# Third batch's normalised rows: transposed by VectorE in 32x32 pieces and brought through DRAM, or by TensorE

## The chip, the cores and the metric

One core of a Trainium2 chip. The time is device microseconds of one launch of the whole kernel. Engines: PE (TensorE, matrix multiply), DVE (VectorE), ACT (ScalarE), POOL (GpSimd) and SP (SyncE, whose queue issues nearly all DMAs here). Each runs its own instructions in order and waits on semaphores for the others.

## What is computed

One transformer block on 4 batches of 512 tokens by 512 features, in float32. Layer normalisation, causal attention with rotary positions (32 query heads of 16 features, 8 key and value heads), a residual, a second layer normalisation, a gated MLP with 1376 hidden features, a second residual.

```python
def reference(resid, Wq, Wk, Wv, Wo, W_gate, W_up, W_down):
    x = resid                                   # (4, 512, 512)
    n = layernorm(x)
    q, k, v = rope(n @ Wq), rope(n @ Wk), n @ Wv
    x = x + softmax(causal(q @ k.T) / 4) @ v @ Wo
    n = layernorm(x)
    return x + (silu(n @ W_gate.T) * (n @ W_up.T)) @ W_down.T
    ...
```

## The kernel before, in words

The kernel writes out the order of every engine's instructions by hand: the Python code runs step by step, and each step appends instructions to the queues. Batches are counted from 0 here, so the third batch is b = 2 and the fourth is b = 3.

*Projections of a batch* (`projections`, L328). A batch's rows come as four tiles of 128 tokens by 512 features, `xa`, by DMA (L338). For each tile:
- `measure` (`statistics`, L196): on DVE the statistics (L200), their aggregate (L201) and the variance plus epsilon (L202), then on POOL the power -1/2 (L203);
- `norm` (`normalised`, L206): for b > 1 a small DVE operation (L210) and the normalisation itself on ACT (L211), in place in `xa`;
- the transposition into `xnT`, which has the features on the partitions, since PE contracts over partitions.

There are two ways to transpose. `transposed` (L255) has PE transpose four blocks of 128x128 into a PSUM bank (L258) and copies the bank to `xnT`, on ACT (L263) or at times on DVE (L261). `flipped` (L265) has DVE transpose all 32x32 blocks of the tile at once into a buffer `xt` (L268; two such buffers), writes it to a DRAM tensor `flip` with the blocks in their places by four DMAs of 64 KB (L272), and reads the columns of the tile before back into `xnT` by one DMA of 256 KB (L274); at the last tile it reads two. All these DMAs are on SP's queue.

Before, batches 0 and 2 go by `transposed` and batches 1 and 3 by `flipped`.

After that come the products on PE: `rest` has 48 portions of four matmuls each or their like (L253): 8 for keys, 8 for the first quarter of the queries, 8 for values, 24 for the other queries. A finished bank is rotated by DVE (a shuffle, L304, and a product, L308) and POOL (L305, L309).

*Attention of a batch* (`slot`). A batch has 8 head groups, and each group is a round of four visits and a last visit. In a visit PE makes scores (L553 and L566) into two pairs of PSUM banks, ACT takes the exponential (L654), POOL applies the causal mask (L659), and DVE finds minima of negated scores for the group two ahead (L599). At the end of a round DVE transposes the minima (L639), SP takes them through DRAM into the masked queries `qa` of a later group (L640, L649, L651), POOL makes the next `qa` (L538), and PE multiplies the exponentials by the values (`averages`, L681).

Between visits, `gap` fills PE with portions from a list of (cost, step): it runs steps until their summed cost reaches the visit's share of the total. Beside it, `odd_steps` takes DVE steps from the queue `aside` as long as a visit's budget of microseconds lasts; `measure`, `norm` and `flip` steps are in that queue. Attention of batch 0 is `slot(0, ...)`, and its list holds the rest of batch 1's products, batch 2's `turned` steps and products, then batch 3's `begin`, `turned` and half of its products. A `turned` step (`tail`) waits in the order of the program until its tile's `flip` step has been taken from `aside`, taking steps if need be, and then calls `transposed` where the batch goes that way.

`begin` of a batch issues the four loads of its rows (unless done) and puts its steps into `aside`. Batch 2's loads are issued earlier, at the end of batch 1's last `flip`; batch 3's are issued where `begin3` stands in the list. The four `xa` buffers are shared: batch 3's rows go into those that batch 2's rows leave.

Of the kernel before, what the change touches and what calls it, by code (L numbers as in the profile page):

```python
# [22 lines left out]
NT = T // P  # L23
# [51 lines left out]
def preln_block_kernel(  # L75
# [65 lines left out]
    def values(n):  # L141

        return homes[n][:, 8:11, :].rearrange("p a c -> p (a c)").rearrange("p (j g d) -> p j g d", j=NT, g=NKV)
# [9 lines left out]
    flip = [dram.tile([D, T], F32, name=f"flip{n}") for n in range(2)]  # L153
# [35 lines left out]
    def put(step):  # L189
        held.append(step) if holding[0] else step()  # L190

    def release():
        while held:
            held.popleft()()

    def statistics(src):  # L196
        st = small.tile([P, 6], F32, tag="st", name="st")
        mv = small.tile([P, 2], F32, tag="mv", name="mv")
        rstd = small.tile([P, 1], F32, tag="rstd", name="rstd")
        nc.vector.bn_stats(st, src)  # L200
        nc.vector.bn_aggr(mv, st)  # L201
        nc.vector.tensor_scalar(rstd, mv[:, 1:2], EPS, None, ALU.add)  # L202
        nc.gpsimd.tensor_tensor(rstd, rstd, neghalf, ALU.pow)  # L203
        return src, mv, rstd

    def normalised(dst, found, by_act=False):  # L206
        src, mv, rstd = found
        if by_act:
            shift = mv[:, 1:2]
            nc.vector.tensor_scalar(shift, mv[:, 0:1], rstd, -1.0, ALU.mult, ALU.mult)  # L210
            put(lambda: nc.scalar.activation(dst, src, AF.Identity, bias=shift, scale=rstd))  # L211
        else:
            nc.vector.tensor_scalar(dst, src, mv[:, 0:1], rstd, ALU.subtract, ALU.mult)
# [3 lines left out]
    aside, later = deque(), deque()  # L217
# [47 lines left out]
    def flipped(xn, i, n, dst, last=NT - 1):  # L265

        t = work.tile([P, D], F32, tag="g", name="xt", bufs=2)
        nc.vector.transpose(t, xn)  # L268
        turned = flip[n].rearrange("(c d) (i r s) -> i r d c s", d=32, r=4, s=32)
        for r in range(4):  # L270
            rows = t[32 * r : 32 * r + 32, :]
            nc.sync.dma_start(out=turned[i, r], in_=rows.rearrange("d (c s) -> d c s", s=32))  # L272
        for a in [i - 1, i] if i == last else [i - 1] if i > 0 else []:
            nc.sync.dma_start(out=dst[:, :, ts(a, P)], in_=flip[n].rearrange("(k p) t -> p k t", p=P)[:, :, ts(a, P)])  # L274
# [24 lines left out]
    def rotated(ps, dst, engine=nc.gpsimd):  # L299

        rot = work.tile([P, T], F32, tag="rot", name="rot", bufs=4)

        def sines():
            nc.vector.stream_shuffle(rot, ps, ROTATE)  # L304
            put(lambda: engine.tensor_tensor(rot, rot, sin, ALU.mult))  # L305

        def cosines():
            nc.vector.tensor_tensor(dst, ps, cos, ALU.mult)  # L308
            put(lambda: engine.tensor_tensor(dst, dst, rot, ALU.add))  # L309

        return [(0.73, sines), (0.69, cosines)]

    def both_steps(measure, norm, flip, tiles=range(NT), norm_us=0.6, flip_us=0.75):

        for i in tiles:
            yield 1.05, lambda i=i: measure(i)
            for a in [i - 1, i] if i == NT - 1 else [i - 1] if i > 0 else []:
                yield norm_us, lambda a=a: norm(a)
                yield flip_us, lambda a=a: flip(a)

    def both_steps_apart(measure, norm, flip, flip_us):

        steps = {"m": (1.05, measure), "n": (0.2, norm), "f": (flip_us, flip)}
        for kind, i in ("m0", "m1", "n0", "m2", "f0", "n1", "m3", "f1", "n2", "n3", "f2", "f3"):
            cost, step = steps[kind]
            yield cost, lambda step=step, i=int(i): step(i)

    def projections(b, n, early=False, then=None):  # L328

        home, xa, found, xn, ready = homes[n], {}, {}, {}, []  # L330
        xnT = xnT_of[b]

        def load(i):
            if early:
                xa[i] = xr[b, i]
            else:
                xa[i] = work.tile([P, D], F32, tag="xa", name="xa", bufs=4)
                nc.sync.dma_start(out=xa[i], in_=x[b, ts(i, P), :])  # L338

        def measure(i):  # L340
            found[i] = statistics(xa[i])

        def norm(i):
            xn[i] = work.tile([P, D], F32, tag="xa", name="xa", bufs=4) if early else xa[i]
            normalised(xn[i], found[i], by_act=b > 1)

        def flip(i):
            if b > 1:
                release()
            if b % 2:  # L350
                flipped(xn[i], i, 1, xnT)
            ready.append(i)
            if i == NT - 1 and then:
                then()

        def keys():
            def finish(ps):
                kr = work.tile([P, T], F32, tag="rot", name="kr", bufs=4)

                def spread():  # L360
                    release()
                    ks = work.tile([P, T], F32, tag="rot", name="ks", bufs=4)
                    nc.vector.stream_shuffle(ks, kr, SWAP)
                    for t, hf, src in ((0, 0, kr), (1, 1, kr), (0, 1, ks), (1, 0, ks)):
                        put(
                            lambda t=t, hf=hf, src=src: nc.gpsimd.tensor_scalar(
                                home[:, 4 + 2 * t + hf, :], src, halves[hf], (one16, one0)[hf], ALU.mult, ALU.add
                            )
                        )

                last = spread if early else lambda: soon.append((1, (0.75, spread)))
                return [*rotated(ps, kr, nc.vector if early else nc.gpsimd), (0.0, last)]

            return projected(wk_sb, 0, xnT, finish)

        def vals():
            def product(ps, i, k):
                for c in (0, 64) if i == NT - 1 else ():
                    token = P * i + 64 - c
                    product_of(  # L380
                        ps[c : c + 64, ts(i, P)], xnT[:, k, token : token + 64], wv_sb[:, k, :], k == 0, k == NK - 1
                    )
                if i < NT - 1:
                    product_of(ps[:, ts(i, P)], xnT[:, k, ts(i, P)], wv_sb[:, k, :], k == 0, k == NK - 1)

            def finish(ps):
                def copy():
                    nc.scalar.copy(
                        values(n)[:, :, :, DH : 2 * DH].rearrange("p i g d -> p (i g) d"),
                        ps.rearrange("p (a d) -> p a d", d=DH),  # L390
                    )

                return [(0.0, copy)]

            steps = [lambda ps, i=i, k=k: product(ps, i, k) for i in range(NT) for k in range(NK)]
            return [(0.45, step) for step in portions(steps, finish, 8)]

        def queries(m):
            engine = nc.vector if early and m == 0 else nc.gpsimd
            return projected(wq_sb, m, xnT, lambda ps: rotated(ps, home[:, m, :], engine))  # L400

        def load_all():
            for i in range(NT):
                load(i)

        def begin():
            if not xa:
                load_all()
            if b > 1:
                aside.extend(both_steps_apart(measure, norm, flip, 0.75 if b % 2 else 0.0))  # L410
            else:
                aside.extend(both_steps(measure, norm, flip, flip_us=0.75 if b % 2 else 0.0))

        def tail(i):
            while i not in ready:
                do(aside)
            if b % 2 == 0:
                transposed(xn[i], i, xnT)

        turned = [(0.0 if b % 2 else 0.45, lambda i=i: tail(i)) for i in range(NT)]  # L420
        rest = [*keys(), *queries(0), *vals()]
        for m in range(1, 4):
            rest += queries(m)
        return (0.0, begin), turned, rest, load_all
# [307 lines left out]

    begin3, turned3, rest3, _ = projections(3, 3)
    begin2, turned2, rest2, load2 = projections(2, 2)
    begin1, turned1, rest1, _ = projections(1, 1, then=load2)
    begin, turned, start, _ = projections(0, 0, early=True)
# [140 lines left out]
    def restored():  # L877
        nc.scalar.dma_start(out=homes[1], in_=spill)

    turns = [step for pair in zip(turned2, *[iter(rest1[-8:])] * 2) for step in pair]  # L880
    slot(0, [*rest1[16:-8], *turns, begin3, *rest2, *turned3, *rest3[:-24]])

    before, behind = attended(0, by_pe=(2, 3))
    tiles = list(down(0, 0))
# [62 lines left out]
```

## Time and profile before

| | |
|---|---|
| median of three runs | 890.2 us (889.15, 890.2, 890.35) |
| the profiled execution: time, span | 889.38 us, 887.7 us |
| granted PE clock | 1.00 |
| PE busy | 865.9 us, 98% of the span |
| DVE, ACT, POOL busy | 469.6, 204.5, 233.7 us |
| PE transposes from `xa` (L258) | 32 of batches 0 and 2, batch 2's between 79.1 and 91.1 us |
| DVE transposes from `xa` (L268) | 8 of batches 1 and 3, from 14.6 to 142.2 us |

Times in a profile are microseconds from the span's start. A timeline line has start, duration, engine, source line, operation, what it writes and reads with shapes, and how many are merged (x4); a bracket at its end is the idle time before it and who released it. SPq is SP's own queue of DMA issues: its durations are those of issuing, not of the transfer. In the chain of waits each piece is what the end of the program waited for at that moment. In a table by stage each row has a stretch A:B, its length, busy time and count of PE, PE's weight loads, DVE, ACT and POOL, then the granted clock, the DMA engines' share and GB/s.

### The profile page before, as it was taken

To read this page: it belongs to the slowest core of one execution; us is meant where nothing else is said; L and a number is where in the kernel's file an instruction comes from. 1 tells how busy PE (TensorE), PEld (TensorE's weight loads), DVE (VectorE), ACT (ScalarE), POOL (GpSimd) and SP (SyncE) were. 2 spreads that over 40 slices of the span, in tenths; PEclk is the share of its full clock that TensorE was granted. 3 is DMA by queue.
4 is the path that set the end of the run, shared out by engine and by line. 5 is a ranking of instruction groups with operands and counts; after the bars stand their busy time and mean duration, and the time that the engine had idled before them with its cause. 6 is when DMAs were issued, how large, how long until landed. Compare 5 with 4: busy or idle time off the path is not lost.

```text
span 887.7 us, 23915 instructions
## 1 busy us (share of the span) xinstructions
PE 865.9 (98%) x10142; PEld 352.0 (40%) x10142; DVE 469.6 (53%) x1481; ACT 204.5 (23%) x256; POOL 233.7 (26%) x358
## 2 busy tenths in 40 slices
PE   6989999999999999999999999999999999999998
PEld 5654444544333333333333333333333334444443
DVE  7886788777555554485555544575555214121110
ACT  1024433322323222222222222122222220000100
POOL 5564475653212211132221122222211211000000
PEclk9999999999999999999999999999999999999999
DMA  8500114005515110524221110142111203523000
GB/s 247 133 5 4 52 16 87 4 4 121 180 50 178 44 50 14 192 51 110 55 57 50 31 40 25 52 98 73 51 50 50 68 13 84 130 71 83 18 13 35
DMA packets 122762, 59.68 MB, mean 67 GB/s; under 512 B 60480, under 2 KB 114752, under 8 KB 122400
## 3 DMA queue, kind: packets, MB, share of 16 engines
q1 hardware_dynamic: 122368, 52.39, 22.7%
q10 hardware_dynamic: 288, 5.77, 1.7%
q8 instruction: 80, 1.31, 0.6%
q14 instruction: 26, 0.21, 0.1%
HBM read 44.76 MB, written 13.37 MB: 65 GB/s over the span
## 4 chain that ended last, share of the span: by engine, by line
PE 81%; DVE 12%; POOL 3%; issue 2%; DMA 1%; ACT 1%; SPq 0%; POOLq 0%; DVEq 0%; ACTq 0%
PE mm L253 42%; PE mm L250 17%; PE sc L553 12%; DVE junk L599 6%; PE av L681 6%; PE sc L566 4%; POOL e L659 1%; DVE st L200 1%; DVE rot L304 1%; POOL qa L538 1%; ACT e L654 1%; DVE home L308 1%; DMA flip<-xt 0%; PE mm L258 0%; DVE xt L268 0%
## 5 line engine op out<-in xcount | busy, mean ns | idle before, releaser
L599 DVE CUSTOM_DVE_ANT_0 junk<-sc,mask 128x128 f32<-128x128 f32 (+3 forms) x512 | 251.1, 490 | 153.5 <-PE sc L566 94.6
L253 PE MATMUL mm<-xnT,shared 128*32 128x512 f32 (+1 forms) x2704 | 282.2, 545 | 1.0 <-DVE xnT L261 1.0
L654 ACT ACTIVATE e<-sc 128x1024 f32<-128x1024 f32 (+1 forms) x192 | 165.5, 882 | 411.7 <-PE sc L566 323.7
L659 POOL TENSOR_SCALAR_AFFINE_SELECT e<-e 128x512 f32<-128x512 f32 (+2 forms) x192 | 105.6, 560 | 365.5 <-ACT e L654 362.6
L553 PE MATMUL sc<-home,qa 32*64 32x512 f32 (+6 forms) x2048 | 158.7, 421 | 5.8 <-DVE low L599 3.0
L566 PE MATMUL sc<-qa,home 32*64 32x512 f32 (+6 forms) x2048 | 152.2, 427 | 2.7 <-DVE low L599 2.2
L253 PEld LDWEIGHTS mm<-xnT,shared 128*32 128x32 f32 x2704 | 88.0, 109 | 157.5 <-issue 142.1
L553 PEld LDWEIGHTS sc<-home,qa 32*64 32x64 f32 x2048 | 67.3, 131 | 109.0 <-issue 40.0
L250 PE MATMUL mm<-xnT,shared 128*128 128x512 f32 (+2 forms) x256 | 94.8, 529 | 0.0
L253 PE MATMUL mm<-wd_sb,home 128*32 128x512 f32 (+1 forms) x808 | 94.7, 594 | 0.0
L681 PE MATMUL av<-e,home 128*32 128x512 f32 (+3 forms) x1024 | 80.6, 437 | 1.4 <-POOL e L659 1.4
L504 DVE SCALAR_TENSOR_TENSOR g<-g,mm 128x512 f32<-128x512 f32 (+1 forms) x44 | 30.2, 687 | 96.6 <-ACT g L503 96.6
L566 PEld LDWEIGHTS sc<-qa,home 32*64 32x64 f32 x2048 | 58.7, 130 | 33.1 <-issue 13.4
L250 PEld LDWEIGHTS mm<-xnT,shared 128*128 128x128 f32 (+1 forms) x256 | 48.0, 190 | 46.6 <-issue 44.7
L503 ACT ACTIVATE g<-mm 128x512 f32<-128x512 f32 (+1 forms) x44 | 26.3, 597 | 168.8 <-PE mm L250 109.6
L250 PE MATMUL mm<-wd_sb,home 128*128 128x512 f32 (+1 forms) x150 | 65.0, 593 | 0.0
L506 DVE TENSOR_TENSOR home<-mm,g 128x512 f32<-128x512 f32 (+1 forms) x44 | 30.4, 690 | 57.3 <-PE mm L253 34.0
L522 DVE SCALAR_TENSOR_TENSOR xr<-mm,xr 128x512 f32<-128x512 f32 x16 | 11.0, 689 | 76.8 <-PE mm L250 56.2
L681 PEld LDWEIGHTS av<-e,home 128*32 128x32 f32 x1024 | 31.1, 109 | 44.8 <-issue 36.6
L253 PEld LDWEIGHTS mm<-wd_sb,home 128*32 128x32 f32 (+1 forms) x808 | 28.2, 110 | 50.6 <-issue 49.6
L253 PE MATMUL mm<-wo_sb,cx 128*32 128x512 f32 x384 | 45.0, 595 | 0.0
L250 PEld LDWEIGHTS mm<-wd_sb,home 128*128 128x128 f32 (+1 forms) x150 | 28.4, 190 | 36.3 <-issue 36.3
(73 smaller groups left out, 452.1 us busy)
## 6 DMA issues: line engine op xcount, KB each, us to landing
shared<-in_wg SPq DMA_DIRECT2D x40, 256.0 KB
shared<-in_wu SPq DMA_DIRECT2D x40, 256.0 KB
flip<-xt SPq DMA_DIRECT2D x88, 64.0 KB
xnT<-flip SPq DMA_DIRECT2D x18, 256.0 KB
xr<-in_x SPq DMA_DIRECT2D x16, 256.0 KB
out<-xr SPq DMA_DIRECT2D x16, 256.0 KB
xa<-in_x SPq DMA_DIRECT2D x12, 256.0 KB
spill<-wd_sb ACTq DMA_DIRECT2D x1, 2816.0 KB
```

The source lines that it names most:

```text
L250: nc.tensor.matmul(out, lhsT=lhsT, rhs=rhs, start=start, stop=stop)
L253: nc.tensor.matmul(out[c : c + 32], lhsT=lhsT[:, c : c + 32], rhs=rhs, start=start, stop=stop)
L503: nc.scalar.activation(gs[f][:m, :], ps[:m, :], AF.Tanh, scale=0.5)
L504: nc.vector.scalar_tensor_tensor(gs[f][:m, :], gs[f][:m, :], 1.0, ps[:m, :], ALU.add, ALU.mult)
L506: nc.vector.tensor_tensor(homes[n][:m, f, :], ps[:m, :], gs[f][:m, :], ALU.mult)
L522: nc.vector.scalar_tensor_tensor(xr[b, i], py[i], 0.5, xr[b, i], ALU.mult, ALU.add)
L553: nc.tensor.matmul(dst[at : at + 64, :n], lhsT=qa[g][rows_of(r), q : q + 64], rhs=keys_of(g)[rows_of(r), :n], start=True, stop=True,)
L566: nc.tensor.matmul(dst[at : at + 64, first_q:], lhsT=keys_of(g)[rows_of(r), k : k + 64], rhs=qa[g][rows_of(r), P * j + first_q :], start=True,
L599: nc.vector.tensor_tensor_reduce(out=junk[:, :n], in0=src, in1=mask[:, T - n : T] if i else mask[:, T:], scale=-1.0, scalar=BIG, op0=ALU.a ...
L654: nc.scalar.activation(dst, src, AF.Exp, scale=1.0 / math.sqrt(DH))
L659: nc.gpsimd.affine_select(out=e[rows, heads, c : c + P], in_=e[rows, heads, c : c + P], compare_op=ALU.is_ge, fill=0.0, base=base, pattern ...
L681: nc.tensor.matmul(av[32 * r : 32 * r + 32, P * j :], lhsT=v[:, j, 4 * (m // 2) + r, DH * (1 - hf) : DH * (3 - hf)], rhs=e[:, r, c : c + n ...
```

## The change

Batch 2 goes by `flipped` too, through the DRAM tensor `flip[0]`. Its `turned` steps cost nothing in the list (they issue no PE work) and stand together, with `begin3` behind them, ahead of the last 12 portions of batch 1's products; before, they were interleaved with the last 8 of those, and `begin3` stood behind these. Batch 2's `flip` steps are given 0.75 us in `aside`, like batch 3's.

```diff
         def flip(i):
             if b > 1:
                 release()
-            if b % 2:
-                flipped(xn[i], i, 1, xnT)
+            if b > 0:
+                flipped(xn[i], i, b % 2, xnT)
             ready.append(i)
...
             if b > 1:
-                aside.extend(both_steps_apart(measure, norm, flip, 0.75 if b % 2 else 0.0))
+                aside.extend(both_steps_apart(measure, norm, flip, 0.75))
             else:
-                aside.extend(both_steps(measure, norm, flip, flip_us=0.75 if b % 2 else 0.0))
+                aside.extend(both_steps(measure, norm, flip, flip_us=0.75 if b else 0.0))
...
         def tail(i):
             while i not in ready:
                 do(aside)
-            if b % 2 == 0:
+            if b == 0:
                 transposed(xn[i], i, xnT)

-        turned = [(0.0 if b % 2 else 0.45, lambda i=i: tail(i)) for i in range(NT)]
+        turned = [(0.0 if b else 0.45, lambda i=i: tail(i)) for i in range(NT)]
...
-    turns = [step for pair in zip(turned2, *[iter(rest1[-8:])] * 2) for step in pair]
-    slot(0, [*rest1[16:-8], *turns, begin3, *rest2, *turned3, *rest3[:-24]])
+    slot(0, [*rest1[16:-12], *turned2, begin3, *rest1[-12:], *rest2, *turned3, *rest3[:-24]])
```

## The prediction

> **What bounds the kernel now.** I read the page's engine totals first, then the chain of work that ended last.
>
> ```profile
> PE 865.9 (98%) x10142; PEld 352.0 (40%) x10142; DVE 469.6 (53%) x1481; ACT 204.5 (23%) x256; POOL 233.7 (26%) x358
> ...
> PE 81%; DVE 12%; POOL 3%; issue 2%; DMA 1%; ACT 1%; SPq 0%; POOLq 0%; DVEq 0%; ACTq 0%
> ```
>
> PE is the bound nearly everywhere: it is idle for 21.8 us of 887.7. So PE time taken out counts in full, and a wait that PE gets counts in full too. The change lies in the attention of batch 0 (about 50 to 178 us), where the busy view gives DVE 7 to 9 tenths: DVE, POOL and PE hand each visit on to one another there. Next the PE timeline around the work removed, and the start of the following head group:
>
> ```profile
> 79.14 0.66 PE L258 MATMUL mm<-ident,xa 128*128 128x128 f32 x4
> 79.73 1.07 PE L253 MATMUL mm<-wd_sb,shared 128*32 128x256 f32 x16
> ...
> 84.16 0.65 PE L553 MATMUL sc<-home,qa 32*64 32x512 f32 x2
> ```
>
> A set of four transposes holds its place for 0.59 us (79.14 to 79.73). Sets stand also at 85.53, 88.19 and 90.76. At 84.16 PE begins the scores of the third head group; that is the mark that I move below.
>
> Then the SyncE queue, where the second batch already went the new way:
>
> ```profile
> 33.93 1.94 SPq L272 DMA_DIRECT2D flip<-xt  x4
> 35.97 1.83 SPq L274 DMA_DIRECT2D wd_sb<-flip  x2
> 37.85 3.72 SPq L338 DMA_DIRECT2D xa<-in_x  x4
> ```
>
> After a batch's last tile come four writes, two reads (the last waits for those writes to land) and only then the next batch's rows. There the first measurement came at 46.15, 8.3 us after the first load was issued, and never waited.
>
> **What goes.** On PE 4 x 0.59 = 2.36 us, of which 0.59 lies before 84.16 and 1.77 behind it. On ACT four copies of 0.58; ACT is busy for 23% and each copy stood in a pause, so I give nothing for them. Three rotating PSUM banks get four claims fewer: nothing.
>
> The Trainium skill, "VectorE: DVE Perf Modes", section "Rules for kernel authors", says that a 128x128 transpose belongs on TensorE where PSUM will do as its destination; that speaks against this change. Its table beside it has 390 ns (TensorE, bf16): 16 of them would be 6.2 us, an estimate by that page, where this trace shows 2.36.
>
> **What comes, on DVE.** Four transposes of 0.70 us: 2.8 us. In the changed program's instruction order the first stands in the first group's fourth visit in place of a measurement (0.69 + 0.18 + 0.15), the second in the second group's second visit in place of a shuffle (0.73): no cost there. The third and fourth stand together behind the third visit (with one 128x1 operation, 0.15): 1.55 us. The nearest row for such a lump is 2 us of side work at 138.5, behind which PE idled 0.84 us at 142.37. Here this is swallowed by the next term; by itself it is 0 to 0.84.
>
> **What comes, on SyncE and behind it.** Sixteen 64 KB writes and four 256 KB reads; at 12 portions of filler (each some 0.5 us, spread over about a group of 15 us) the reads are covered for PE. The order of what follows is the point. Batch 3's four loads are queued right behind the last read, and the measurement of its first tile (L200) stands on DVE in the *same* group, after the fourth visit's eight minima and ahead of a shuffle, a product and the last visit's minima. DVE is in order; so is POOL, where that tile's reciprocal root (L203) stands ahead of the second group's last two causal masks (L659) and the next mask of queries (L538). PE needs all of these before 84.16's scores. So whoever waits for the load holds up all three.
>
> Step by step, in the old clock:
> - Second transpose at 74.49 (end of that visit's minima) to 75.2; its four writes take 1.94 to 2.08 on the queue: 77.2; a read of 0.48: 77.7.
> - Third transpose behind the minima that end at 77.49: 77.65 to 78.35; writes to 80.4; read to 80.9.
> - Fourth: needs ACT's normalisation (0.81, from 77.65) and the second tile's writes landed (two buffers): about 78.5 to 79.2. Its writes queue until 80.9 and take until 82.9.
> - The two reads: 1.83 us (opening) to 3.11 us (at 145.07, fourth batch). First load issued at 84.8 to 86.1; I take 85.3, nearer the quiet opening.
> - Issue to landed. Batch 3's old loads show the bounds:
>
> ```profile
> 89.11 2.70 SPq L338 DMA_DIRECT2D xa<-in_x  x4
> ```
> ```profile
> 90.00:91.00 1.00, 1.00 (x34) 0.69 (x26) 0.45 (x2) 0.00 (x0) 1.00 (x2) 1.00 0.63 172
> 91.00:92.00 1.00, 1.00 (x16) 0.59 (x18) 0.96 (x3) 0.93 (x2) 0.05 (x1) 1.00 0.91 350
> 92.00:93.00 1.00, 1.00 (x24) 0.44 (x24) 0.69 (x6) 0.57 (x2) 0.00 (x0) 1.00 1.15 326
> 93.00:94.00 1.00, 1.00 (x36) 0.61 (x32) 0.06 (x1) 0.00 (x0) 0.00 (x0) 1.00 0.51 182
> ```
>
> The last column is GB/s. A quarter of the 1.05 MB has moved by 91.3, all of it by 94: 2.2 to 4.9 us after the issue. I take 3.9, since the four share 16 engines and the first ends with its slowest piece.
> - So the measurement starts at 89.2 (87.0 to 91.0); DVE gets there at about 81.5, after the fourth visit's 1.8 us of minima. A wait of some 7.7 us.
> - From such a measurement to the next group's scores, the trace has the same sequence one group later; the measurement there starts at 95.69:
>
> ```profile
> 97.15 0.55 POOL rstd L203
> 97.70 0.37 POOL e L659
> ...
> 98.51 0.70 POOL qa L538
> ...
> 99.26 0.64 PE sc L553 x2
> ```
>
> That is 3.57 us. DVE's own way (1.0 measure, 1.3 shuffle and product, 0.9 two minima) is 3.2, just shorter. PE's scores start at 92.8 (90.6 to 94.6) and not at 84.16: 8.6 late (6.4 to 10.4). PE's cover in the meantime, the filler, the last visit and the averages, is what it did in the old clock too.
>
> **Two small terms.** PE idled 0.55 us at 95.82 behind a visit with three filler portions; four stand there in the changed order, and the fourth batch's transposes are no longer paired with a rotation (0.84 at 142.37): -0.5 taken, 0 to -1.4. And PE stands still for about 7 us. The only such pause in the trace is the start, 6.23 us long, and behind it:
>
> ```profile
> 6.23 1.11 PE L258 MATMUL mm<-ident,xa 128*128 128x128 f32 x4 [6.23 <-DVE xa L213]
> 7.73 1.11 PE L258 MATMUL mm<-ident,xa 128*128 128x128 f32 x4 [0.39 <-DVE xa L213]
> ```
>
> Four transposes took 1.11 there, 0.66 later, although the granted clock is given as 1.00 in both places; this lasted to about 11 us. Five us at that pace lose 5 x (1 - 0.66/1.11) = 2.0. I add 0.7 of 0 to 2.0, since behind the stall PE also waits for DVE.
>
> The Trainium skill, "TensorE: Matmul & The Clock Gate", section "HAM oscillation — how this bites in real kernels", has the array fall to half clock after more than some 3.4 us idle; 3.4 us at half speed would be 1.7 us, an estimate by that page, and the sum 1.0 higher.
>
> **Sum.** 8.6 - 1.77 - 0.5 + 0.7 = 7.0. The profiled execution took 889.4 us (span 887.7): 896.4. The median, 890.2, lies 0.8 above that execution: 897.2. Ends: 6.4 - 1.77 - 1.4 = 3.2, so 893.4; 10.4 - 1.77 + 2.0 = 10.6, so 900.8; with half of a lump's 0.84, 901.3.
>
> **Rivals.**
> - *Not slower: the load is there in time.* Then only the 2.36 us count: 887.8. It needs the first load landed by about 81.5, so issued by 78 or so; the fourth tile's transpose is not even read out by then. It also comes if PE does not need what is queued behind the measurement, which the order on POOL speaks against. 0.07.
> - *No change that shows.* No long wait, but DVE's 2.8 us lengthen up to four visits at up to 0.84 each: -2.4 + 0 to 3.4, 888 to 891.2; taken 890. Decides if the wait is under 2 us. 0.04.
> - *A short stall*, 2 to 3 us lost, if the reads wait less and the loads land at once: 892.5. 0.04.
> - *A longer one.* The queue runs at its worst pace for both pairs of tiles (four writes took 3.07 at 136.24, against 2.0): 2 us more, and the slow start costs its full 2: 903. 0.05.
>
> The forecast has 0.80. A measurement of this kernel tells about 0.2% (1.8 us) from no change. Slower by more than that: 0.80 + 0.04 + 0.05 = 0.89; within it 0.04; faster 0.07. The range 893.0 to 901.5 leaves out the four rivals, 0.20.
>
> **What would show it.** In the changed profile: no L258 after 12 us apart from the eight near 214; an L200 on `xa` around 81 us with a DVE idle of 6 to 9 us, released by DMA `xa<-in_x`; a PE idle of 6 to 8 us before a score or an average near 85; the load issued by SyncE near 85, right behind two `xnT<-flip`. After that the groups run some 1.8 us faster than before in all. I am wrong if DVE has no idle of over 2 us ahead of that L200, if PE's pause is not released through POOL L203, L659 or DVE L599, or if the loss lies after 178 us.

## The result, and the profile after

The changed kernel takes 899.1 us (median; 898.6 to 900.5) against 889.7 us for the kernel before beside it: ratio 1.0109, 95% interval [1.0094, 1.0123], 9.4 us slower. The forecast of 897.2 (893.0 to 901.5) holds; the loss is 2.4 us larger than its 7.0.

The profile below is of an execution of 900.48 us, the longest of those measured; a second profiled execution of the same kernel comes further down. The engine totals and the chain of work that ended last, from the page of the changed kernel:

```profile
PE 865.8 (96%) x10126; PEld 350.8 (39%) x10126; DVE 472.2 (53%) x1485; ACT 202.6 (23%) x252; POOL 233.1 (26%) x358
...
PE 82%; DVE 10%; POOL 2%; DMA 2%; issue 2%; SPq 1%; ACT 0%; POOLq 0%; DVEq 0%; ACTq 0%
```

Sixteen PE transposes are gone (10142 to 10126), and PE is idle for 33.0 us instead of 21.8. Its busy time has hardly changed, though: in the first two experiments below, which have no stall, it is 863.1 and 862.8, and here the matmuls behind the stall take longer. DMA and SyncE's queue have larger shares of the chain (2% and 1%, from 1% and 0%). SyncE's issues in the attention of batch 0, from the timeline of the changed kernel:

```profile
74.50 2.98 SPq L272 DMA_DIRECT2D flip<-xt  x4
...
83.31 3.79 SPq L274 DMA_DIRECT2D xnT<-flip  x2
87.15 1.93 SPq L338 DMA_DIRECT2D xa<-in_x  x4
```

Four writes of the second tile, two reads behind the last tile, and right behind them batch 3's loads, at 87.15. In the chain of waits the last write is followed by 4.0 us of transfer (`flip<-xt`, 82.66 to 86.67): the last read waits for it to land. DVE in the same timeline (the bracket is the idle time before the instruction and its releaser):

```profile
79.08 0.71 DVE L268 STREAM_TRANSPOSE xt<-xa 128x512 f32<-128x512 f32 x1 [1.49 <-DMA flip<-xt]
...
90.27 0.69 DVE L200 BATCH_NORM_STATS2 st<-xa 128x6 f32<-128x512 f32 x1 [8.75 <-DMA xa<-in_x]
```

DVE waits 8.75 us for the first of these rows. POOL, then PE:

```profile
91.52 0.55 POOL L203 TENSOR_TENSOR rstd<-rstd,neghalf 128x1 f32<-128x1 f32 x1 [10.37 <-DVE rstd L202]
92.03 0.77 POOL L659 TENSOR_SCALAR_AFFINE_SELECT e<-e 128x256 f32<-128x256 f32 x2
92.78 0.69 POOL L538 TENSOR_SCALAR qa<-home,rope_sb 128x512 f32<-128x512 f32 x1
```
```profile
81.58 0.69 PE L566 MATMUL sc<-qa,home 32*64 32x256 f32 x16 [1.79 <-DVE low L599]
...
92.49 1.43 PE L681 MATMUL av<-e,home 128*32 128x256 f32 x8 [8.04 <-POOL e L659]
93.85 1.12 PE L553 MATMUL sc<-home,qa 32*64 32x512 f32 x2
...
96.42 2.74 PE L253 MATMUL mm<-wd_sb,shared 128*32 128x256 f32 x24
```

POOL stands at L203 for 10.37 us with the last two masks (L659) and the next queries (L538) behind it; PE stands for 8.04 us, and the third group's scores begin at 93.85, not 84.16. The last line is another loss: the same 24 matmuls take 1.50 us at full clock.

### The profile page after: what moved, and what is told of

Its sections match the earlier page's. It is cut to its first block, busy times and chain, and to the rows that moved or that the text cites. A ratio compares the mean times of both kernels' runs of the same rounds, so it can differ in the third digit from the quotient of the medians.

```text
span 898.8 us, 23912 instructions
## 1 busy us (share of the span) xinstructions
PE 865.8 (96%) x10126; PEld 350.8 (39%) x10126; DVE 472.2 (53%) x1485; ACT 202.6 (23%) x252; POOL 233.1 (26%) x358
## 4 chain that ended last, share of the span: by engine, by line
PE 82%; DVE 10%; POOL 2%; DMA 2%; issue 2%; SPq 1%; ACT 0%; POOLq 0%; DVEq 0%; ACTq 0%
PE mm L253 41%; PE mm L250 19%; PE sc L553 12%; DVE junk L599 7%; PE av L681 6%; PE sc L566 4%; POOL e L659 1%; DMA flip<-xt 1%; SPq L272 1%; DVE st L200 1%; POOL qa L538 1%; DMA xr<-in_x 1%; DVE rot L304 0%; DVE home L308 0%; ACT e L654 0%
## 5 line engine op out<-in xcount | busy, mean ns | idle before, releaser
L659 POOL TENSOR_SCALAR_AFFINE_SELECT e<-e 128x512 f32<-128x512 f32 (+2 forms) x192 | 105.3, 558 | 364.5 <-ACT e L654 361.6
L681 PE MATMUL av<-e,home 128*32 128x512 f32 (+3 forms) x1024 | 80.8, 439 | 8.9 <-POOL e L659 8.9
L681 PEld LDWEIGHTS av<-e,home 128*32 128x32 f32 x1024 | 31.0, 109 | 52.3 <-issue 37.7
L203 POOL TENSOR_TENSOR rstd<-rstd,neghalf 128x1 f32<-128x1 f32 x32 | 20.4, 637 | 90.1 <-DVE rstd L202 89.9
```

Source lines behind the costliest of these rows:

```text
L659: nc.gpsimd.affine_select(out=e[rows, heads, c : c + P], in_=e[rows, heads, c : c + P], compare_op=ALU.is_ge, fill=0.0, base=base, pattern ...
L681: nc.tensor.matmul(av[32 * r : 32 * r + 32, P * j :], lhsT=v[:, j, 4 * (m // 2) + r, DH * (1 - hf) : DH * (3 - hf)], rhs=e[:, r, c : c + n ...
```

## The experiments

Each kernel differs from the changed one by the diff shown, unless its text says otherwise (lines that only hand a function or a buffer through are left out), and is compared with the kernel before on the same chip; where a number is called the end of a group, it is the end of the group's averages (L681) on PE.

**Is it the load?** Batch 3's first two tiles come early, into a part of `xnTs[1]` that is free then, so that only the other two loads stand behind the reads. The order of all steps is the changed kernel's.

```diff
-    xa[i] = work.tile([P, D], F32, tag="xa", name="xa", bufs=4)
+    xa[i] = xnTs[1][:, i, :] if b == 3 and i < 2 else work.tile([P, D], F32, tag="xa", name="xa", bufs=4)
...
-    ... = projections(1, 1, then=load2)
+    ... = projections(1, 1, then=lambda: (load2(), load3(0), load3(1)))
```

> The changed kernel with every DVE and PE instruction in the same order; only the loads of batch 3's first two tiles are issued with batch 2's loads, into rows of the second xnT that are free until then. The measurement at its old place then finds its tile. Theory A (the wait for the load on DVE, and the slow PE clock behind it, are the whole loss): the 8.8 us wait and the half clock go, the PE transposes stay away; about 888 us (887 to 890). Rival B (the third and fourth DVE transposes, their buffer wait and DVE's 2.8 us are what lengthens the visits): 894 to 898. Rival C (the 2 MB of small DMA pieces slow every transfer): 894 to 899.

Measured: 889.07 us against 889.74, ratio 0.9995 [0.9986, 1.0004]. DVE comes to L200 at 81.62 and finds its rows there. Its timeline:

```profile
79.27 0.71 DVE L268 STREAM_TRANSPOSE xt<-xa 128x512 f32<-128x512 f32 x1 [1.40 <-DMA flip<-xt]
...
81.62 0.69 DVE L200 BATCH_NORM_STATS2 st<-xnT 128x6 f32<-128x512 f32 x1
```

The two reads take 3.87 us here too (83.37), and nothing waits for what stands behind them. The whole loss hangs on rows that are late for that one measurement.

**Is it the place of the measurement?** The loads stay where the change has them; batch 3's steps go behind the twelve portions.

```diff
-    ..., *turned2, begin3, *rest1[-12:], *rest2, ...
+    ..., *turned2, (0.0, load3), *rest1[-12:], begin3, *rest2, ...
```

> The changed kernel with batch 3's loads at their new place, right behind the last read, but its measuring steps entered only behind the 12 portions, a head group later. Theory A: the load is as late as in the changed kernel, yet nobody waits for it: no DVE idle for a load, PE clock 1.00 throughout, 887 to 890 us. Rival C (the transfers themselves, or the full queue, cost the time): 894 to 899, since queue and transfers are unchanged.

Measured: 889.29 us against 889.74, ratio 0.9995 [0.9986, 1.0004]. The loads are issued at 86.87, as late as in the changed kernel, and nothing waits for them. Either cure alone undoes the loss, so it needs both: the late load and the early measurement. That the queue and its transfers cost time by themselves is ruled out too, since they are unchanged here.

**Is the order of the list enough?** The kernel before, with PE's transposes, in the changed order.

```diff
-    turns = [step for pair in zip(turned2, *[iter(rest1[-8:])] * 2) for step in pair]
-    slot(0, [*rest1[16:-8], *turns, begin3, *rest2, *turned3, *rest3[:-24]])
+    slot(0, [*rest1[16:-12], *turned2, begin3, *rest1[-12:], *rest2, *turned3, *rest3[:-24]])
```

> The kernel before, with PE's transposes of batch 2, and only the list's order of the changed kernel: the turned steps together and begin3 behind them, ahead of the last twelve portions. Three sets of transposes then stand on PE ahead of the second group's fourth visit, the fourth set behind it; batch 3's loads wait only for these to read the rows, so they are issued between 77 and 81 and landed by 84 at the latest. Theory (the stall needs the way through DRAM: two reads queue ahead of the loads on SyncE): DVE does not wait for xa<-in_x by over 0.5 us, scores of the third group at 84 to 86, time 889.3 to 891.0 (up to 1 us for the three sets without products between, since their banks are emptied one by one). Rival (the order of the list alone puts the measurement too early, whatever brings the rows): DVE waits 3 us or more at L200, 892 to 898.

Measured: 891.35 us against 890.17, ratio 1.0013 [1.0004, 1.0022]. PE's timeline, then one line of DVE's:

```profile
77.43 0.66 PE L258 MATMUL mm<-ident,xa 128*128 128x128 f32 x4
78.76 1.41 PE L258 MATMUL mm<-ident,xa 128*128 128x128 f32 x8 [0.68 <-ACT xnT L263]
```
```profile
89.39 0.69 DVE L200 BATCH_NORM_STATS2 st<-xa 128x6 f32<-128x512 f32 x1
```

The loads are issued at 78.19, 9 us before those of the changed kernel, and DVE does not wait for rows. But the measurement stands elsewhere too, behind the first visit of the third group and not in the second group. So the order of the list alone makes no stall; what a measurement in the second group would have met on PE's way is not shown. The time is 0.35 us above the range that was expected, and the third group's scores (86.55) 0.55. The first three groups end 1.3, 2.4 and 3.3 us later than in the kernel before. Three sets in a row wait for ACT to empty a bank (0.68 us), and the second and third groups are 1.1 and 0.9 us longer; the 1.3 of the first group lies ahead of the sets and is not explained. In this order PE's way loses 1.2 us.

**Is it the queue?** Batch 3's loads on ACT's queue instead of SyncE's.

```diff
-    nc.sync.dma_start(out=xa[i], in_=x[b, ts(i, P), :])
+    (nc.scalar if b == 3 else nc.sync).dma_start(out=xa[i], in_=x[b, ts(i, P), :])
```

> The changed kernel with batch 3's four loads issued from ACT's queue in place of SyncE's, so that they do not stand behind the writes and reads of batch 2. Theory A with the queue as the cause of the late load: the first load is issued near 79 to 80 and lands at 83 to 85, DVE waits 2 to 4 us in place of 8.8, PE's pause stays under some 4 us; 889 to 893 us. If the load itself, not its place in the queue, is what is late: DVE waits 7 us or more, 896 to 899. The price: ACT waits for the fourth transpose before it issues the last load, and an exponential stands behind that.

Measured: 890.83 us (889.31 to 894.17) against 889.74, ratio 1.002 [1.0008, 1.0032]. ACT's queue and ACT:

```profile
76.62 4.88 ACTq L338 DMA_DIRECT2D xa<-in_x  x4
81.55 1.02 ACT L654 ACTIVATE e<-sc 128x1024 f32<-128x1024 f32 x1 [4.12 <-DVE xt L268]
```

The first load is issued at 76.62, earlier than expected, and DVE doesn't wait at L200 (82.78) at all, so the two reads ahead on SyncE were what made the load late. The wait moved: ACT's queue is in order as well, and its exponential now stands behind loads that wait for the fourth DVE transpose to leave `xa`. PE is idle for 3.53 us ahead of 82.91. Most of the loss is undone, and a new one of 1.1 us stands in its place. The eleven executions fall into two sets: seven of 889.3 to 891.1 us with a mean granted clock of 1.00, the profiled one among them, and four of 893.0 to 894.2 with 0.996. None of the four was profiled; that the clock fell behind PE's pause there is likely, not shown.

**Where did the 2.36 us of PE go?** With the stall gone the time should have fallen by them; in the first two experiments it fell by 0.7 and 0.45, neither clear of noise (both intervals include 1). PE's waits from 50 to 222 us (waiting instruction, what it waited for, us, times, longest) in the kernel before, then in the kernel with the steps later, and one line each of the latter's DVE and PE timelines:

```profile
PE sc L553 <- DVE low L599: 2.3, 4, 0.7
PE sc L566 <- DVE low L599: 2.2, 3, 0.8
```
```profile
PE sc L553 <- DVE low L599: 5.0, 9, 0.7
PE sc L566 <- DVE low L599: 3.4, 3, 1.9
```
```profile
78.97 0.71 DVE L268 STREAM_TRANSPOSE xt<-xa 128x512 f32<-128x512 f32 x1 [1.57 <-ACT e L654]
```
```profile
81.46 0.69 PE L566 MATMUL sc<-qa,home 32*64 32x256 f32 x16 [1.87 <-DVE low L599]
```

From 2.3 and 2.2 us the two waits grew to 5.0 and 3.4: PE's time was swapped for idle time. One part is 1.87 us ahead of the second group's last visit, where the fourth DVE transpose has a pause of 1.57 us before it. The other is waits of some 0.55 us at visits with two portions of filler: with the sets gone from the list there are more such visits (nine waits against four), and there DVE's minima decide, not PE. First, the steps and the loads of batch 3 both behind the portions, and nothing else (in its text e3 is the kernel with the steps later and e9 the next one below):

```diff
-    ..., *turned2, begin3, *rest1[-12:], *rest2, ...
+    ..., *turned2, *rest1[-12:], begin3, *rest2, ...
```

> The changed kernel with only begin3 moved behind the twelve portions (loads and steps of batch 3 both), the two shared xt buffers kept. It stands between two kernels already run: as e9 without the own buffers, and as e3 but with the loads later too. Theory (what was left to lose after the stall is the 1.6 us wait of the fourth DVE transpose for a buffer and an activation, which puts 1.9 us of PE idle ahead of the last visit): the wait and the PE idle of 1.7 to 1.9 us stay, 889.0 to 889.6, and the own buffers of e9 bring 1.2 us. Rival (e9's gain came from loading batch 3 later, at 91.8 and not at 86.9, so that its loads don't meet batch 2's flips): 887.8 to 888.4 as e9, whatever the PE idle shows. No DVE wait for xa<-in_x in either.

Measured: 888.91 us against 890.17, ratio 0.9995 [0.9986, 1.0004]. The fourth transpose waits 1.44 us (for DMA `flip<-xt`) and PE 1.74. The median lies just below the first range (889.0 to 889.6) and above the rival's (887.8 to 888.4); three of the eleven executions took 890.6 to 891.5 at a mean clock of 0.997, without a profile that would show why. The traces are clearer: the second group takes 16.71 us against 16.83 with only the steps later, and groups three to eight 92.04 against 91.99. A later load is not what helps. Next, batch 2's DVE transposes go into a free part of `xnTs[1]` instead of the two shared `xt` buffers:

```diff
-    flipped(xn[i], i, b % 2, xnT)
+    flipped(xn[i], i, b % 2, xnT, t=xnTs[1][:, i, :] if b == 2 else None)
...
-    ..., *turned2, begin3, *rest1[-12:], *rest2, ...
+    ..., *turned2, *rest1[-12:], begin3, *rest2, ...
```

> begin3 behind the 12 portions, so that nobody waits for its loads, and the DVE transposes of batch 2 each into a buffer of its own (free rows of the second xnT) in place of two shared ones. Theory A': the PE time saved (2.36 us) was eaten by PE's idle time of 1.7 to 1.9 us ahead of the last visit, which comes from the third and fourth transposes standing together with a wait between them; without the buffer wait the fourth still waits for ACT (about 0.2 to 0.5), PE's idle there falls to 0.5 to 0.9, and the time is 0.6 to 1.3 us below the kernel with the steps later (889.3): 888 to 888.7. Rival: the wait of the fourth transpose is ACT's, behind an exponential, and own buffers change nothing: 889 to 889.5.

Measured: 888.09 us against 889.97, ratio 0.9979 [0.997, 0.9989]. DVE's and PE's timelines:

```profile
77.17 0.71 DVE L268 STREAM_TRANSPOSE xnT<-xa 128x512 f32<-128x512 f32 x1 [0.26 <-ACT xa L211]
```
```profile
79.66 0.69 PE L566 MATMUL sc<-qa,home 32*64 32x256 f32 x16 [0.56 <-DVE low L599]
```

The fourth transpose waits 0.26 us, PE 0.56 instead of 1.74, and the second group takes 15.53 us instead of 16.71 in the experiment above: the wait for a buffer was worth 1.2 us. Last, the third and the fourth transpose go to visits of their own:

```diff
-    slot(0, [*rest1[16:-12], *turned2, begin3, *rest1[-12:], *rest2, ...])
+    slot(0, [*rest1[16:-12], *turned2[:2], *rest1[-12:-8], turned2[2], *rest1[-8:-5], turned2[3], *rest1[-5:], begin3, *rest2, ...])
```

> As the kernel with own buffers, but the last two turned steps are entered 4 and 7 portions later, so that the fourth transpose stands behind the fourth visit's minima and not beside the third's. Theory A': no lump, PE's idle ahead of the last visit under 0.9 us, and most of the 2.36 us is kept: 887.3 to 888.5, below the kernel before (889.7). Rival: DVE's total (2.8 us more) is the bound in these visits, wherever its pieces stand: 889 to 889.8.

Measured: 887.44 us (887.03 to 888.06) against 889.97, ratio 0.9971 [0.9959, 0.9982]: 2.5 us faster than the kernel before and 11.4 faster than the changed one on the same chip. PE's waits from 50 to 222 us:

```profile
PE sc L553 <- DVE low L599: 5.0, 9, 0.7
PE sc L566 <- DVE low L599: 1.6, 2, 0.8
```

The lump ahead of the last visit is gone, and the second group takes 15.09 us, as undisturbed ones do, against 16.23 in the kernel before. The nine short waits stay: groups three to eight take 92.39 us against 92.19, so nothing is gained there. The two profiled spans are 2.0 us apart (885.7 and 887.7): 1.1 of it lies in the second group, 0.6 behind the tenth, where nothing was edited, and 0.5 ahead of the end of the first.

**What did the slow clock cost?** PE is kept busy through its pause with 44 matmuls by zeros added to the averages, then the changed kernel again, then 32 of them.

```diff
+    for z in range(44 if g == 1 and j == 2 else 0):   # then 32
+        r = z % 4
+        nc.tensor.matmul(av[32 * r : 32 * r + 32, :], lhsT=mask[:, 0:32], rhs=e0[:, r, :], start=False, stop=False)
```

> The changed kernel with 44 matmuls against a block of zeros added into the averages of the second group, ahead of the part that waits for POOL: the sum is the same, and PE works through most of the pause (some 6.6 us of 8.0). The DVE wait stays at 8.8 us. If the half clock behind the pause costs PE time: the clock stays at 1.00 and the time falls by 2 to 3.5 us, 895.5 to 897.5. If the half clock is hidden under DVE's work behind the stall, or costs what the forecast took (0.7): 898 to 899.5.

> The changed kernel once more, beside the others of this set on the same chip: 898.6 to 900, DVE's wait for the load near 8.8 us, the clock at 0.50 for some 10 us behind it.

> As the kept-warm kernel, with 32 matmuls in place of 44: they took 0.215 us each, so 6.9 us in place of 9.5, which ends before POOL is ready and so delays nothing. In that run PE's next block of 24 matmuls took 1.50 us against 2.74 in the changed kernel. If the half clock costs what these rows show (1.43 against 0.99, 2.5 against 1.3, 2.74 against 1.50), the time is 2 to 3 us below the changed kernel's in this set; if it is hidden behind DVE, under 0.8 us below.

Measured: with 44, 898.53 us against 889.74 (ratio 1.01 [1.0086, 1.0114]), but they end at 92.5, some 1.5 us after the averages could have gone on (its L200 at 88.80, and 2.2 us from there to the averages as in the changed kernel). With 32: 898.35 against 889.97 (1.0091 [1.0075, 1.0106]); the changed kernel beside it: 898.88 (1.01 [1.0086, 1.0113]). In the profiled executions the clock stays at 1.00 over the pause with either; in the kernel with 32, in PE's timeline:

```profile
83.91 7.05 PE L682 MATMUL av<-e,mask 128*32 128x512 f32 x64
...
94.98 1.50 PE L253 MATMUL mm<-wd_sb,shared 128*32 128x256 f32 x24
```

The difference of 0.5 us lies inside the intervals: the slow clock is seen, but its price in the median is not settled. Two of the four executions with 32 have a mean clock of 0.998 and took 898.7 and 898.8; the one at 1.00 took 896.9. The price differs between executions, too. The third group takes 17.24 us in the first profile of the changed kernel and 16.13 in the second, against 15.09 where nothing stalls (steps later): 2.1 and 1.0 us. Against the kernel with 32, which has the same order and the same stall at full clock (15.71), it is 1.5 and 0.4. In the second profile DVE's wait is 8.22 us (8.8 expected), and the clock is at 0.50 for 6.8 us, not the 10 that were expected from the first.

## Why the forecast was right, and where it was not

- **What bounds, and the wait that takes over**: as forecast. Load behind two reads, L200 early on DVE, POOL held at L203 with what PE needs behind it. From L200 to the third group's scores it took 3.58 us (forecast 3.57), but that they agree so closely is luck. POOL was done with L538 3.20 us after L200 began (93.47); in the forecast's row it was 3.51, since L203 still stood behind earlier masks there. In its place PE's eight matmuls of averages took 1.43 us at half clock, not 0.99. In the kernel with 32, at full clock, the same way is 3.27 (89.73 to 93.00). That two separate cures each undo the loss shows the mechanism. The rival "load in time" fell on the point it had named: the fourth tile was not read out by 78.
- **The queue was mis-sized**, in the two reads above all: they took 3.79 us, where 85.3 rests on 2.4 (82.9 to 85.3) and 3.11 was the upper bound. The second tile's four writes took 2.98 us, not 2.0, but had begun 0.7 earlier than forecast (74.50); the fourth tile's were issued by 83.15, only 0.25 late. The first load was issued at 87.15, not 85.3, outside 84.8 to 86.1. The landing made up for a part: 3.1 us after the issue, not 3.9. So the measurement stood at 90.27 (forecast 89.2), the wait was 8.75 us (7.7), and the scores were 9.69 us late (8.6). In the second execution, nearest to the median, it comes closer: issued at 86.50, measured at 89.49, a wait of 8.22, scores at 93.07, which is 8.91 late; the group's end is 9.04 late (93.15 against 84.11).
- **The step that failed is "PE time taken out counts in full"**, the term of -1.77 with the -0.5 beside it. From the end of the second group to the end of the eighth the kernel before needs 92.19 us and the kernel with the steps later, which has no stall, 91.99: 0.2 gained, not 2.3. PE was busy for 98% of the span, but in this stage DVE's minima set the length of a visit as soon as its filler is short, and PE's time turns into waits of 0.55 us. (The busy view's digits for DVE there are 6 to 8, not 7 to 9, and 6 in the slice from 66.6 to 88.8 us, where the change begins: even so DVE ends some visits last.) The part that can be got lies elsewhere: in the second group, by buffers and spreading.
- **The -0.5 by itself**: the idle of 0.84 at 142.37 did go (in the changed kernel PE has no idle there; with the steps later it is back, 0.84 at 142.93), but new idles of 0.56, 0.94 and 0.56 stand at 101.77, 117.68 and 120.68.
- **The slow start** was taken at 0.7 of 0 to 2.0. Two executions show 2.1 and 1.0 in the third group, and 0.4 more in the eight matmuls of averages (1.43 against 0.99); against the kernel with 32 the third group shows 1.5 and 0.4. The medians differ by 0.5, which is not clear of noise, so whether PE's waits for others hide the rest, as had been argued, stays open.
- **The sum with what was measured**, in the second execution (898.73 us, nearest to the median): the second group's end 9.04 late; groups three to eight +0.80 (0.2 gained and 1.0 lost behind the stall, about half of it at full clock too: 92.52 us with 32 matmuls, 91.99 with the steps later); the next two groups +0.1; the rest of the program -0.6. That is +9.3, and 889.38 + 9.3 = 898.7.
- **The lump of two DVE transposes** (0 to 0.84, swallowed by the stall): it costs 1.2 to 1.9 us of PE idle in every kernel with the two shared buffers and SyncE's loads, with the stall or without it, because a wait of 0.9 to 1.6 us lies inside it, which own buffers cut to 0.26.
- **The Trainium skill**, "VectorE: DVE Perf Modes", section "Rules for kernel authors", has 128x128 transposes belong on TensorE where PSUM will do as their destination. The spread version disagrees for this case: through DVE and DRAM it is 2.5 us faster than the kernel before, with 1.1 us of it traced to the second group. PE's way was not tried with batch 3's steps as late as there.

Open: from the end of the tenth group to the end the kernel before takes 665.75 us and the variants that go through DRAM about 665.15, but 665.42 with the loads on ACT's queue; the kernel with PE's way in the new order takes 665.45. Nothing there was edited and no experiment was made on it.

## What to carry to other kernels

A transposition through DRAM costs its own engines little, but on an in-order queue everything issued behind its last read comes late (here 8.1 us after the last transpose began, 79.08 to 87.15); put the first consumer of such a load at least a round behind it on *every* in-order engine, and count what stands behind that consumer, not the consumer itself. Before counting removed PE time as a gain, look whether PE's idle times in that very stage are already released by another engine: if so, the gain can turn into longer waits, as in groups three to eight here, where no variant gained more than 0.6 of the 1.8 us. Small buffers shared between producers (two `xt` here) can be the whole difference between no measurable change (ratio 0.9995) and a gain (0.9979).

## What the hardware showed that was not expected

The granted clock fell during PE's pause and stayed down after it. The changed kernel's table by stage (stretch, length, busy time and count of PE, PE's weight loads, DVE, ACT, POOL, granted clock, DMA share, GB/s):

```profile
86.00:88.00 2.00, 0.00 (x0) 0.00 (x0) 0.00 (x0) 0.00 (x0) 0.00 (x0) 1.00 0.48 140
88.00:90.00 2.00, 0.00 (x0) 0.00 (x0) 0.00 (x0) 0.00 (x0) 0.00 (x0) 0.68 0.88 295
90.00:92.00 2.00, 0.00 (x0) 0.00 (x0) 1.66 (x6) 0.00 (x0) 0.48 (x1) 0.50 0.91 309
...
98.00:99.00 1.00, 1.00 (x12) 0.20 (x4) 1.00 (x2) 0.00 (x0) 0.30 (x1) 0.51 0.02 3
99.00:100.00 1.00, 1.00 (x20) 0.23 (x16) 0.20 (x1) 0.00 (x0) 0.98 (x1) 1.00 0.03 4
```

PE ends its work at 84.45. The mean of 0.68 in the second stretch puts the fall to 0.50 at about 88.7, some 4 us later. PE resumes at 92.49, and full clock is back at about 99.0, 6.5 us after that. In the second execution the same pause (PE resumes at 91.72) is over sooner: the clock is 0.50 until 95 and 0.77 from 95 to 96, so it is back after 3.7 us:

```profile
95.00:96.00 1.00, 1.00 (x16) 0.29 (x12) 0.28 (x1) 0.17 (x1) 0.85 (x2) 0.77 0.00 0
```

A pause of 3.53 us (loads on ACT's queue, profiled execution) left the clock at 1.00.

The Trainium skill, "TensorE: Matmul & The Clock Gate", section "HAM oscillation — how this bites in real kernels", has the array at half clock after more than some 3.4 us idle. The fall agrees with it (0.50, some 4 us after PE's last work); the return took 3.7 us once and 6.5 us once. The pause of 3.53 us shows that a gap just beyond that length need not bring the fall.
